# One-hot products a step ahead of the sums, and batch norm's operands loaded early, in the expert block of a four-block Flamingo kernel

## The chip, the cores and the metric

The kernel runs on one core of one Trainium2 chip. The metric is the device time of one execution in microseconds. The profiled execution, the source of all views below, is a separate run with a time of its own. The engines are called as the profile calls them: PE does matrix products, DVE and POOL elementwise work, ACT functions and copies, SP issues most of the DMAs.

## The reference, cut to what matters

The input is x of 8 sequences by 512 tokens by 256 features, with a context of the same shape. Four blocks follow each other: an mLSTM cell across to the context, a 32-head self-attention with a mixture of experts, a 16-head cross attention, and the block that the change is about, a feed-forward layer of 4096 tiny experts chosen by product keys:

```python
q = jnp.einsum('bnd,de->bne', x, w_q)
mean = jnp.mean(q, axis=(0, 1))
var = jnp.var(q, axis=(0, 1))
q = (q - mean) * jax.lax.rsqrt(var + BN_EPS) * bn_gamma + bn_beta
q = q.reshape(b, n, 2, H, KD).transpose(2, 0, 1, 3, 4)
sim = jnp.einsum('pbnhd,hkpd->pbnhk', q, keys)
sx, ix = jax.lax.top_k(sim[0], TOPK)
sy, iy = jax.lax.top_k(sim[1], TOPK)
all_scores = (sx[..., :, None] + sy[..., None, :]).reshape(b, n, H, TOPK * TOPK)
all_indices = (ix[..., :, None] * NUM_KEYS + iy[..., None, :]).reshape(b, n, H, TOPK * TOPK)
scores, pk = jax.lax.top_k(all_scores, TOPK)
indices = jnp.take_along_axis(all_indices, pk, axis=-1)
wd = down_embed[indices]
wu = up_embed[indices]
h = jnp.einsum('bnd,bnhkd->bnhk', x, wd)
h = gelu_new(h)
h = jax.nn.softmax(scores, axis=-1) * h
out = jnp.einsum('bnhk,bnhkd->bnd', h, wu)
```

H is 8, TOPK 8, NUM_KEYS 64, so a token takes 64 of 4096 experts. In front of the layer x is layer-normed, and behind it its result is scaled by the tanh of a gate and added to x. Batch norm's mean and variance run over all tokens of all sequences, so no key can be compared before the last token's features exist.

## The kernel before

Tokens come in 32 tiles of 128, and in 16 blocks of 256 (two tiles). The first 3153 us are the attention phase, blocks 1 to 3, one sequence after the other in the order 0, 4, 1, 5, 2, 6, 3, 7. There a small planner on the host interleaves lanes of work, by credits, beside the attention heads. Its last part for each sequence is `leave`: it writes x to x_d, transposes the normed features, stores them to xT_d, and adds to `gram`, the sum over tokens of feature times feature with a column of sums beside it. A lane `inner` computes, for every token of a sequence that has left and for all 4096 experts, the product of the features with `down` (`expert_products`, L123), and stores it to h_d. For the last sequence this is done in block 4. The two blocks of this last sequence are the first that block 4 works on.

Block 4 doesn't gather rows. It weighs all 4096 experts for each token, with zeros for those not chosen, and has two parts.

`fold_phase` (L1145 to L1280) makes the keys. From `gram` and w_q it takes the mean and mean square of each of the 2048 queries (y L1199, sq L1208: products of z = y times w_q with a column of ones), then a scale and shift per query (bn_sc, the power on POOL L1221), and multiplies them into the keys (ks L1226, kh L1228). pw (L1256) is w_q times these keys, copied to mk; pc (L1232) is the constant, kept in crow. From then on a similarity needs only features times mk plus crow. Between these stand the pieces of `activations`: products of the last sequence's features with four rows of down (dwl, L123 into ps_hl), and their gelu on ACT into gs. Its operands lie in up_sb, the 64 KB per partition that later hold `up`, the second table of the experts; as they are used up, `up` is loaded over them.

The step loop (L1372 on) has 128 steps (p, u): tile p, and u one of its four groups of 16 columns; eight steps make a block. The parts that a tile passes through are:

- `similar` (L1062): PE makes the similarities of a tile in two halves from features loaded from xT_d, ACT copies them to sim (L1064).
- `top` (L1075, L1076): DVE takes the eight largest of 64 for each of 16 lists, with their places. `choose` (L1082 to L1096): DVE adds the two lists, takes the eight largest of 64 again, ACT takes the exponentials. `places` (L1106 to L1142): the chosen numbers and weights, as one-hot sums on DVE, with copies on ACT (iv, kf, mlw); PE transposes them (tr), ACT copies that into ciT and cwT.
- `one_hot` (L1303 to L1309), per step: DVE writes two tables of zeros and ones (o1, o2), ACT copies the first (m1), POOL multiplies the second by the weights (m2). Each of these four has two buffers.
- `weights_of` (L1319): PE multiplies m2 by m1 into cf, the weights of all 4096 experts. `weigh` (L1328): DVE multiplies cf into gs, the activations of this block.
- `finish` (L1337): PE sums gs times up_sb over the experts, 64 rows for a block, into acc; `store` (L1352) adds x and writes out.
- `fetch` (L1360) loads a quarter of the products of the next block but one from h_d into gs, of which there are two; `apply` (L1366) takes their gelu on ACT.

Only PE's instructions are in the order of the program. DVE's, ACT's, POOL's and SP's are set by the scheduler from the order of the calls and from its own estimates. In the fold phase SP's are in program order too. In the step loop a step makes, in this order, cf of its own step, the one-hot tables of the next one, a chunk of the sums of the block before, and the weighing. Then, for a later tile, top in steps 0 and 1, choose in 2, places in 3, similar in 2 and 3, and so on for the second tile.

Of the kernel before, what the change touches and what calls it, by code (L numbers as in the profile page):

```python
# [21 lines left out]
P = 128  # L22
# [14 lines left out]
def kernel(  # L37
# [43 lines left out]
    nc.scalar.activation(tg, tg, AF.Tanh)  # L81

# [45 lines left out]

    def attention_phase(ctx: ExitStack):
# [3 lines left out]
        trp = ctx.enter_context(tc.tile_pool(name="trp", bufs=1))  # L133
        cxp = ctx.enter_context(tc.tile_pool(name="cxp", bufs=1))
        prb = ctx.enter_context(tc.tile_pool(name="prb", bufs=4))
        cel = ctx.enter_context(tc.tile_pool(name="cel", bufs=2))
        row = ctx.enter_context(tc.tile_pool(name="row", bufs=1))
        osb = ctx.enter_context(tc.tile_pool(name="osb", bufs=1))
        wmp = ctx.enter_context(tc.tile_pool(name="wmp", bufs=1))
        wsp = ctx.enter_context(tc.tile_pool(name="wsp", bufs=2))  # L140
        exp = ctx.enter_context(tc.tile_pool(name="exp", bufs=2))
# [22 lines left out]
        class Weights:  # L164


            def __init__(self, name, uses):
                self.name, self.uses, self.next = name, list(uses), None
                self.fetch()

            def fetch(self):
                self.next = None
                if self.uses:
                    w, i = self.uses.pop(0)
                    self.next = wsp.tile([P, NK, D], F32, name=self.name, tag=self.name)
                    nc.sync.dma_start(self.next, w[i].rearrange("(k p) n -> p k n", p=P))
# [7 lines left out]
        weights1 = Weights("ws1", M * [(w0, 0), (w0, 1), (w0, 2)])  # L184
        operand = [(w0, 3), (w3, 1), (w3, 0)]
        weights2 = Weights(
            "ws2", (M - 2) * (operand + [(w3, 2)]) + 2 * operand + 2 * [(w3, 2)]
# [270 lines left out]
        def cell(m):  # L458
            b = order[m]
            qn = tok.tile([P, NC, D], F32, name="qn", tag="t1")  # L460
# [64 lines left out]
            hk = tok.tile([P, NC, D], F32, name="hk", tag="t1")  # L525
# [92 lines left out]
        def queries(m):  # L618
            xn = tok.tile([P, NC, D], F32, name="xn", tag="t1")
# [39 lines left out]
        def experts(m):  # L659
# [8 lines left out]
            x2 = tok.tile([P, NC, D], F32, name="x2", tag="t2")  # L668
# [57 lines left out]
        def operands(m):  # L726
            Xb, cT = xbs[m][:, :, :D], cTs[m]
            b = order[m]
            xn = tok.tile([P, NC, D], F32, name="xn3", tag="t2")
# [43 lines left out]
        def leave(m):  # L773
# [4 lines left out]
            yield ("rest", ("H", m - 1))  # L778
            oT = exp.tile([P, NK, S], F32, name="oT3", tag="xT", bufs=1)
# [12 lines left out]
            xT4 = xTs[m] = exp.tile([P, NK, S], F32, name="xT4", tag="xT", bufs=1)  # L792
            yield from to_features(xT4, Xb)
            nc.sync.dma_start(xT_d[:, :, b * S : (b + 1) * S], xT4)
# [72 lines left out]
        def behind():  # L867
            for m in range(M):
# [3 lines left out]
                ready.add(("C", m, 0))  # L872
                for n in (m,) if m < M - 2 else (m - 1, m) if m == M - 1 else ():
                    yield ("rest", ("C", n - 1, 0))
                    yield from values1(n)
                    ready.add(("v1", n))
# [140 lines left out]
    p2 = ctx.enter_context(tc.tile_pool(name="p2", bufs=1))  # L1017
    NB = NT // 2
    up_sb = p2.tile([P, 64, D], F32, name="up_sb")
# [25 lines left out]
    tk = ctx.enter_context(tc.tile_pool(name="tk", bufs=2))  # L1045
    oh = ctx.enter_context(tc.tile_pool(name="oh", bufs=2))
    ps_t = ctx.enter_context(tc.tile_pool(name="ps_td", bufs=2, space=PSUM))

    sims, tops, chosen, cts, hots, accs = {}, {}, {}, {}, {}, {}

    def similar(p, h):

        if h == 0:
            t = tiles[p]
            xt = tk.tile([P, NK, P], F32, name="xTt")
            nc.sync.dma_start(xt, xT_d[:, :, t * P : (t + 1) * P])
            sims[p] = (xt, tk.tile([P, 16, 64], F32, name="sim"))
# [87 lines left out]
    def fold_phase(ctx: ExitStack):  # L1145

        wp = ctx.enter_context(tc.tile_pool(name="wp", bufs=2))
        st = ctx.enter_context(tc.tile_pool(name="st", bufs=1))
        ps_h = ctx.enter_context(tc.tile_pool(name="ps_hl", bufs=2, space=PSUM))
        ps_y = ctx.enter_context(tc.tile_pool(name="ps_yf", bufs=2, space=PSUM))  # L1150
        ps_s = ctx.enter_context(tc.tile_pool(name="ps_st", bufs=1, space=PSUM))

        def room(i, shape):

            axes = dict(zip("ab", shape))
            return up_sb[:, 4 * i : 4 * i + 4, :].rearrange(
                "p x y -> p (x y)"
            ).rearrange("p (a b) -> p a b", **axes)

        xl = room(15, (NK, S))  # L1160
        nc.sync.dma_start(xl, xT_d[:, :, last * S : (last + 1) * S])
        bn_sb = st.tile([P, 32], F32, name="bn_sb")
        nc.scalar.dma_start(bn_sb, bn)
        wqs = [room(n4, (NK, 512)) for n4 in range(4)]
        for n4, wq in enumerate(wqs):
            nc.scalar.dma_start(
                wq, pwq[:, 512 * n4 : 512 * (n4 + 1)].rearrange("(k p) n -> p k n", p=P)
            )
        kT = room(14, (16, 64))
        nc.scalar.dma_start(kT, keysT)  # L1170
        wTs = [room(6 + i, (4, D)) for i in range(4)]
        for i, wT in enumerate(wTs):
            nc.scalar.dma_start(wT, pwqT[:, 4 * i : 4 * i + 4, :])

        def activations(i4):

            dw = wp.tile([P, NK, 4, 64], F32, name="dwl")
            nc.sync.dma_start(dw, down[:, :, 4 * i4 : 4 * i4 + 4, :])
            for i2 in range(2):
                ps = ps_h.tile([P, 2, 2 * P], F32, name="ps_hl")  # L1180
# [265 lines left out]
```

## Time and profile before

| | us |
|---|---|
| median of 3 runs (lowest, highest) | 4202.37 (4200.03, 4207.3) |
| the profiled execution, its time | 4210.22 |
| its span | 4208.4 |
| attention phase, ends at | 3153.4 |
| fold phase, to the first one-hot product | 182.4 |
| first block, to the first store | 93.2 |
| 13 blocks, 53.4 each | 694.6 |
| last two blocks | 84.8 |

Over the span PE is busy 87%, DVE 55%, ACT 41% and POOL 14%, with a mean granted PE clock of 0.936. A time of a row in the profile is that of one instruction or group; a wait is read as "who waits, on which line, for whom". Busy shares of the whole span say little about block 4, for it is a quarter of the time and DVE is its second full engine.

### The profile page before, as it was taken

The page shows a single profiled execution, that of the slowest core. Times are in us where ns is not written, and L with a number is a line of the kernel's source. Part 1 is how long each engine was busy: PE and PEld are TensorE (multiplying, and loading weights), DVE is VectorE, ACT ScalarE, POOL GpSimd, SP SyncE. Part 2 cuts the span into 40 slices and gives each one's busy share as a digit, 9 for nine tenths or more (in the row PEclk, how much of TensorE's full clock was granted, in tenths as well). Part 3 has the DMA queues.
Part 4 walks back from the last instruction along what each step waited for, and adds up shares of the span by engine and source line. Part 5 has one row for each costly group of instructions (what it writes and reads, how often), then busy time and mean ns, then how long its engine had stood idle before and what let it go on. Part 6 is the DMA issues. An engine that isn't in the chain of part 4 may idle for free.

```text
span 4208.4 us, 75108 instructions
## 1 busy us (share of the span) xinstructions
PE 3661.8 (87%) x30633; PEld 1884.0 (45%) x30633; DVE 2332.0 (55%) x5610; ACT 1730.6 (41%) x2290; POOL 604.0 (14%) x611
## 2 busy tenths in 40 slices
PE   5588888889989989998989998788998589999998
PEld 2222343434334344434434434234445367777776
DVE  3465654455555455455545534554203488888984
ACT  2124443334544453453454443443431244554541
POOL 3210102020011012002100200100000122222221
PEclk7578999999999999999999999999998799999999
DMA  3201122123114213311421421102242422222221
GB/s 100 50 26 41 30 63 67 50 69 104 57 56 127 78 59 106 106 39 57 130 74 44 119 82 38 37 24 76 94 127 74 103 80 90 96 97 96 97 96 34
DMA packets 197477, 314.86 MB, mean 75 GB/s; under 512 B 24510, under 2 KB 149982, under 8 KB 188830
## 3 DMA queue, kind: packets, MB, share of 16 engines
q1 hardware_dynamic: 178844, 248.39, 20.0%
q0 software_dynamic: 15616, 56.63, 4.5%
q10 hardware_dynamic: 2672, 5.04, 0.4%
q8 instruction: 241, 3.95, 0.4%
q14 instruction: 104, 0.85, 0.1%
HBM read 220.93 MB, written 88.24 MB: 73 GB/s over the span
## 4 chain that ended last, share of the span: by engine, by line
PE 69%; DVE 19%; DMA 4%; issue 4%; ACT 2%; POOL 1%; SPq 0%; DVEq 0%; POOLq 0%; ACTq 0%
PE sc L333 21%; PE ps_hd L123 9%; PE acc L1337 9%; DVE nm L351 8%; PE av L394 6%; PE ps_y L710 3%; PE ps_p L282 3%; PE ps_q L293 3%; PE ps_h L693 3%; PE csc L567 2%; PE cav L552 2%; PE ps_sim L1062 1%; DVE gs L1328 1%; PE cf L1319 1%; PE ps_hl L123 1%
## 5 line engine op out<-in xcount | busy, mean ns | idle before, releaser
L351 DVE TENSOR_REDUCE nm<-sc 128x2 f32<-128x1024 f32 x768 | 939.7, 1225 | 1020.6 <-PE sc L333 1016.9
L379 ACT ACTIVATE pr<-sc 128x1024 f32<-128x1024 f32 x768 | 785.1, 1023 | 1043.5 <-PE sc L333 1041.8
L333 PE MATMUL sc<-ka,qa 32*128 32x512 f32 x3072 | 938.7, 673 | 216.4 <-DVE nm L351 201.8
L333 PE MATMUL sc<-qa,ka 32*128 32x512 f32 x3072 | 897.4, 657 | 22.7 <-ACT pr L379 11.4
L333 PEld LDWEIGHTS sc<-ka,qa 32*128 32x128 f32 x3072 | 256.4, 191 | 626.4 <-DVE nm L351 431.2
L1337 PE MATMUL acc<-up_sb,gs 64*128 64x256 f32 x4096 | 493.0, 396 | 39.3 <-DVE gs L1328 39.3
L1337 PEld LDWEIGHTS acc<-up_sb,gs 64*128 64x128 f32 x4096 | 407.3, 196 | 95.7 <-DVE gs L1328 41.4
L123 PE MATMUL ps_hd<-xT,dw 128*64 128x256 f32 x3584 | 432.2, 385 | 4.8 <-DVE pd L572 2.1
L394 PE MATMUL av<-pr,v 128*32 128x512 f32 x3072 | 427.2, 629 | 4.7 <-ACT pr L379 4.7
L123 PEld LDWEIGHTS ps_hd<-xT,dw 128*64 128x64 f32 x3584 | 244.9, 137 | 231.6 <-issue 105.8
L1309 POOL TENSOR_TENSOR m<-o,cwT 128x1024 f32<-128x1024 bf16 x128 | 244.3, 1909 | 693.5 <-PE cf L1319 444.9
L333 PEld LDWEIGHTS sc<-qa,ka 32*128 32x128 f32 x3072 | 242.3, 187 | 68.9 <-issue 33.6
L826 ACT COPY hb<-ps_hd 128x512 f32<-128x512 f32 x224 | 130.7, 585 | 293.3 <-PE ps_hd L123 279.3
L545 ACT ACTIVATE pd<-mb,aT 128x512 f32<-128x512 f32 (+3 forms) x256 | 129.7, 553 | 206.3 <-PE cav L552 94.8
L394 PEld LDWEIGHTS av<-pr,v 128*32 128x32 f32 x3072 | 61.5, 109 | 310.4 <-issue 292.0
L537 POOL TENSOR_SCALAR_AFFINE_SELECT mb<-mb 128x256 f32<-128x256 f32 x128 | 52.2, 408 | 864.5 <-DMA mb<-nM_d 439.8
L1319 PE MATMUL cf<-m,m 64*64 64x64 f32 x8192 | 152.6, 222 | 23.6 <-DVE gs L1328 23.5
L572 DVE SCALAR_TENSOR_TENSOR pd<-csc,pd 128x512 f32<-128x512 f32 (+3 forms) x256 | 115.6, 484 | 95.8 <-PE csc L567 72.0
L1328 DVE TENSOR_TENSOR gs<-cf,gs 128x1024 f32<-128x1024 f32 x128 | 154.7, 1209 | 15.4 <-PE cf L1319 15.4
L1319 PEld LDWEIGHTS cf<-m,m 64*64 64x64 f32 x8192 | 135.8, 135 | 58.8 <-issue 54.6
L567 PE MATMUL csc<-qT,cT 32*128 32x256 f32 (+3 forms) x512 | 148.8, 561 | 12.5 <-DVE pd L572 9.0
L1075 DVE MAX8 s<-sim 128x8 f32<-128x64 f32 x512 | 91.1, 210 | 117.0 <-ACT sim L1064 117.0
(225 smaller groups left out, 4212.5 us busy)
## 6 DMA issues: line engine op xcount, KB each, us to landing
h_d<-hb SPq DMA_DIRECT2D x224, 256.0 KB
gs<-h_d SPq DMA_DIRECT2D x56, 1024.0 KB
dw<-in_down SPq DMA_DIRECT2D x112, 256.0 KB
w1e<-in_w POOLq DMA_DIRECT2D x16, 1024.0 KB, 5.5
w2e<-in_w POOLq DMA_DIRECT2D x16, 1024.0 KB, 6.0
mb<-nM_d SPq DMA_DIRECT2D x32, 512.0 KB
qk_d<-pk SPq DMA_DIRECT2D x64, 256.0 KB
ws<-in_w SPq DMA_DIRECT2D x56, 256.0 KB
```

Source lines behind the costliest of these rows:

```text
L123: nc.tensor.matmul(ps[64 * q : 64 * q + 64, :], dw[:, k, :], runs[:, :, q, :], start=(k == 0), stop=(k == NK - 1),)
L333: nc.tensor.matmul(sc[:, i, :], lhs[r : r + 32, g, c * P : (c + 1) * P], rhs[r : r + 32, g, :], start=True, stop=True,)
L351: newest = nc.vector.tensor_reduce(self.nm[:, c, 2 * half : 2 * half + 2, g], sc, AX.X, ALU.max, negate=True)
L379: nc.scalar.activation(self.pr[jj], sc, AF.Exp)
L394: nc.tensor.matmul(self.av[32 * j : 32 * j + 32, :], self.va[:, c, h * (self.hd + 1) : h * (self.hd + 1) + 32], pr[j // 2][:, j % 2, :], s ...
L545: nc.scalar.activation(pds[c][:, i, s0:], mb[:, i, s0:], AF.Exp, bias=aT[:, c, h : h + 1])
L567: nc.tensor.matmul(sc[i][:, s0:], cT[r : r + 32, g, s0 : s0 + P], qT[r : r + 32, g, s0:], start=True, stop=True,)
L826: nc.scalar.copy(hb.rearrange("p n i t -> p i n t"), ps.rearrange("p i (n t) -> p i n t", n=2),)
L1309: nc.gpsimd.tensor_tensor(m2, o2, tokens(cw), ALU.mult)
L1319: nc.tensor.matmul(cf[64 * q : 64 * q + 64, h, s, :], m2[rows, 4 * q + s // 2, :, s % 2], m1[rows, 4 * q + s // 2, :, s % 2], start=True, ...
L1328: nc.vector.tensor_tensor(gv, cf.rearrange("p h s i -> p i h s"), gv, ALU.mult)
L1337: nc.tensor.matmul(accs[n][q], gs[n % 2][rows, i, :], up_sb[rows, i, :], start=(i == 0), stop=(i == 63),)
```

## The change

Of the attention phase: the pools that are used only early move to the other end of SBUF, and are closed when the last sequence's operands are made. The room is given at once to up_sb, and SP loads into it w_q in both layouts (pwq, pwqT), the keys and four pieces of down. The last sequence's transposed features are written straight to their place in up_sb, rather than to xT_d and back, and its last part no longer waits for the expert products of the sequence before it. `bn` is loaded at the start.

Of the fold phase: y is made with the queries in rows (32 products of 128x257, w_q stationary, gram moving). DVE multiplies by the other layout and reduces, so that the 64 products sq with a column of ones are gone; ACT copies the mean column. The expert products come in 32 pieces that are put between the other steps as fill, with down loaded four pieces ahead, into rows 48 to 55 of up_sb. ps_hl and y have three PSUM buffers instead of two. Two more tiles' worth of similarities are made here (tiles 2 and 3). Pools in block 4 wait for a buffer tile by tile.

Of the step loop: the one-hot tables are made two steps ahead, and cf one step ahead of the step that weighs it. PE then has cf of the next step, then a chunk of sums. Top, choose and places of a block's two tiles come in the block before, and their similarities at steps 6 and 7 of the block before that, with the features loaded at steps 3 and 4. Fetches are at steps 1, 2, 4 and 5, gelus at 3, 4, 6 and 7, the store at step 6, and the sums are cut differently.

```diff
+    class Fold:
+        def load(self):
+            pool = ctx.enter_context(tc.tile_pool(name="ups", bufs=1, side="right"))
+            self.up = pool.tile([P, 64, D], F32, name="up_sb")
+            self.xl = self.room(15, (NK, S))
+            self.wqs = [self.room(n4, (NK, 512)) for n4 in range(4)]
+            for n4, wq in enumerate(self.wqs):
+                nc.sync.dma_start(
+                    wq, pwq[:, 512 * n4 : 512 * (n4 + 1)].rearrange("(k p) n -> p k n", p=P)
+                )
+            self.wTs = [self.room(6 + i, (4, D)) for i in range(4)]
+            for i, wT in enumerate(self.wTs):
+                nc.sync.dma_start(wT, pwqT[:, 4 * i : 4 * i + 4, :])
+            self.kT = self.room(14, (16, 64))
+            nc.sync.dma_start(self.kT, keysT)
+            self.dws = {}
+            for i4 in range(4):
+                self.fetch(i4)
...
@@ leave @@
-            yield ("rest", ("H", m - 1))
+            if m < M - 1:
+                yield ("rest", ("H", m - 1))
+                oT = exp.tile([P, NK, S], F32, name="oT3", tag="xT", bufs=1)
+            else:
+                oT = fold.room(10, (NK, S))
...
+            else:
+                yield from to_features(fold.xl, Xb)
@@ behind @@
+                if m == M - 1:
+                    early.close()
+                    fold.load()
@@ fold_phase @@
+        mv = st.tile([P, 16, 2], F32, name="mv")
+        for n4 in range(4):
+            z = room(4 + n4 % 2, (4, D))
+            for i in range(4):
+                n = 4 * n4 + i
+                y = ps_y.tile([P, 512], F32, name="y", tag="y")[:, : D + 1]
+                for k in range(NK):
+                    nc.tensor.matmul(
+                        y, fold.wqs[n4][:, k, i * P : (i + 1) * P], gram[:, k, :],
+                        start=(k == 0), stop=(k == NK - 1),
+                    )
+                nc.vector.tensor_tensor(z[:, i, :], y[:, :D], wTs[n4][:, i, :], ALU.mult)
+                nc.scalar.copy(mv[:, n, 1:2], y[:, D : D + 1])
+            nc.vector.tensor_reduce(mv[:, 4 * n4 : 4 * n4 + 4, 0], z, AX.X, ALU.add)
+        fill(4)
...
         for h in range(2):
+            pw = [ps_y.tile([P, 8, 64], F32, name="pw", tag="y") for _ in range(NK)]
...
+            fill(2)
+            similar(0, h)
+            top(0, 8 * h)
+        values(2, 0, 1, 3, 4)
+        for h in range(2):
+            similar(1, h)
+        choose(0)
+        fill(6)
+        places(0)
+        values(5)
+        for h in range(2):
+            top(1, 8 * h)
+        choose(1)
         for h in range(2):
             similar(2, h)
+        fill(8)
+        for h in range(2):
+            similar(3, h)
+        places(1)
+        fill(32)
+        values(6, 7)
@@ the step loop, all of it @@
-    one_hot(0, 0)
-    cuts = (0, 11, 22, 33, 44, 54, 64)
-    for p in range(NP):
-        n = p // 2
-        for u in range(4):
-            step = 4 * (p % 2) + u
-            cf = weights_of(p, u)
-            if p + u // 3 < NP:
-                one_hot(p + u // 3, (u + 1) % 4)
-            if n > 0 and step < 6:
-                finish(n - 1, cuts[step], cuts[step + 1])
-            weigh(p, u, cf)
-            if p + 2 < NP:
-                if u < 2:
-                    top(p + 2, 8 * u)
-                elif u == 2:
-                    choose(p + 2)
-                else:
-                    places(p + 2)
-            if p + 3 < NP and u >= 2:
-                similar(p + 3, u - 2)
-            if n > 0 and step == 5:
-                store(n - 1)
-            if n > 0 and n + 1 < NB and step in (2, 3, 4, 5):
-                fetch(n + 1, step - 2)
-            if n > 0 and n + 1 < NB and step >= 4:
-                apply(n + 1, step - 4)
+    cuts = (0, 11, 22, 33, 44, 55, 64, 64, 64)
+    steps = [(p, u) for p in range(len(tiles)) for u in range(4)]
+    for step in steps[:2]:
+        one_hot(*step)
+    ahead = weights_of(*steps[0])
+    for g, (p, u) in enumerate(steps):
+        n, step = g // 8, g % 8
+        cf, ahead = ahead, weights_of(*steps[g + 1]) if g + 1 < len(steps) else None
+        weigh(p, u, cf)
+        if n > 0:
+            finish(n - 1, cuts[step], cuts[step + 1])
+        if g + 2 < len(steps):
+            one_hot(*steps[g + 2])
+        if n > 0 and step == 6:
+            store(n - 1)
+        if n + 1 < NB:
+            q = 2 * n + 2 + step // 4
+            if u < 2:
+                top(q, 8 * u)
+            elif u == 2:
+                choose(q)
+            else:
+                places(q)
+        if n + 2 < NB:
+            if step in (3, 4):
+                features(2 * n + 1 + step)
+            if step >= 6:
+                for h in range(2):
+                    similar(2 * n - 2 + step, h)
+        if n > 0 and n + 1 < NB:
+            if step in (1, 2, 4, 5):
+                fetch(n + 1, (1, 2, 4, 5).index(step))
+            if step in (3, 4, 6, 7):
+                apply(n + 1, (3, 4, 6, 7).index(step))
```

## The prediction

> **What bounds the kernel now.** I read busy time by windows first. The page's slices end in a stretch where DVE goes to 8 and 9 tenths; I cut it where block 4 begins (first product of dwl, 3153.4), at the first one-hot product (3335.8), at the first store's sum (3429.0) and before the last two blocks (4123.6).
>
> ```profile
> core 0: us, PE busy (x) PEld busy (x) DVE busy (x) ACT busy (x) POOL busy (x), PEclk, DMA share, GB/s
> 3153.40:3335.80 182.40, 126.50 (x776) 78.91 (x776) 56.33 (x237) 35.41 (x92) 8.32 (x5) 0.80 0.40 102
> 3429.00:4123.60 694.60, 640.58 (x10306) 490.39 (x10302) 613.93 (x2549) 346.98 (x519) 197.95 (x104) 0.96 0.29 95
> ```
>
> The fold phase is a third idle on PE, with its clock at 0.80. The steady loop is 13 blocks of 53.4 us, PE 92% and DVE 88% busy: both are nearly full. Next the waits, first of the fold phase:
>
> ```profile
> POOL bn_sc L1221 <- DVE bn_sc L1220: 65.7, 1, 65.7
> PE ps_hl L123 <- DMA dwl<-in_down: 25.1, 2, 15.9
> PE ps_sim L1062 <- DMA xTt<-xT_d: 15.5, 1, 15.5
> ```
>
> PE stands for transfers: of dwl 25.1 us, of the features xTt 15.5 us. Then the waits of the loop (3480 to 4120, 12 blocks):
>
> ```profile
> ACT gs L1366 <- DMA gs<-h_d: 41.8, 17, 4.6
> PE acc L1337 <- DVE gs L1328: 33.4, 12, 2.8
> PE cf L1319 <- DVE gs L1328: 14.4, 12, 1.2
> ```
>
> Per block PE waits 2.8 us once for the last weighing, and 1.2 once. The timeline of PE shows the place and what follows:
>
> ```profile
> 3641.49 1.19 PE L1319 MATMUL cf<-m,m 64*64 64x64 f32 x64 [1.20 <-DVE gs L1328]
> ...
> 3649.11 8.07 PE L1337 MATMUL acc<-up_sb,gs 64*128 64x256 f32 x44 [2.79 <-DVE gs L1328]
> ```
>
> 44 sums take 8.07 us after that wait, 4.95 at full clock (the same 44 elsewhere in that timeline): the window 3648.5 to 3655.3 has clock 0.50. So a block is 256 sums 28.8 + 8 cf x 1.12 = 9.0 + four similarity products 8.8 + two tr 0.8 = 47.4, waits 4.0, lost clock 2: 53.4.
>
> Last, DVE and POOL together:
>
> ```profile
> 3585.13 1.90 POOL L1309 TENSOR_TENSOR m<-o,cwT 128x1024 f32<-128x1024 bf16 x1 [3.79 <-ACT gs L1366]
> 3585.64 1.47 DVE L1129 TENSOR_TENSOR mlw<-w,sm 128x64 f32<-128x64 f32 x1
> ```
>
> The 128x64 product takes 1.47 us here and 0.23 alone: it ends when POOL's product does.
>
> **What the Trainium skill says.** "SBUF — State Buffer", section "Who interferes with whom": a DVE instruction with two SBUF inputs and a GpSimd instruction that reads SBUF block each other for a whole instruction. The pair above agrees. "TensorE: Matmul & The Clock Gate", Part 1: an idle window of 3.4 us halves the clock. Here waits of 2.8 us already brought 0.50, for 6.8 us and in another block for 3.4 us. Same page, "Engine queue depths": ACT and DVE are strictly first in, first out; the order below rests on it. "Trainium Kernel Development and Optimization", "Key Constraints": queues of different engines share the 16 DMA engines, so a transfer isn't faster for coming from another queue. Agrees: dwl is waited for while the ups move at 221 to 233 GB/s.
>
> **The change part by part.** *Loads in the attention phase.* Now 5.6 MB are issued on SP at about 2876; at 190 to 237 GB/s (the trace's heavy stretches) 24 to 30 us, ahead of the last ws, xT_d and h_d on SP. Those come due over 25 us later; their order on all engines is the same up to the last leave. I take 0, bounds 0 and +5 (beyond that, the fourth rival). The last element's transposed features stay on chip, which removes its store and reload, hence the 15.5, and its transposes stand before 72 expert products: block 4 begins 1.2 us sooner.
>
> *Fold phase, PE at full clock.* y: 64 rows x 0.26 (ps_g, same form) 16.7. Thirty-two pieces of expert products (8 of L123) at 1.88: 60.2. pw 7.4, pc twice 0.9, eight similarity products at 2.2 = 17.6, two tr 0.8. Sum 104.5 (before 126.5 busy at a mean clock of 0.80, with six similarity products). The 64 small sums of squares are gone; the 4 reductions and 16 column copies on DVE and ACT are under y. The chain bn_sc to ks (POOL's pow 2.9, ks 1.1, five small ones) is about 5.5, covered by four pieces (7.5). Down pieces are fetched four deep; the ninth and tenth of 256 KB queue behind 5.2 MB of ups (22 to 25 us), of which the eight pieces and two products in front hide all but 6.6. Other stalls (ACT's copies, choose and places ahead of tr) 4. Half clock after them 3. Sum 118: first cf at 3152.2 + 118.5 = 3270.7, so 65 earlier than 3335.8. Bounds 105 (no stalls) and 140 (ups at 150 GB/s).
>
> *First block.* Its sums end after one block of steps with DVE in front (50, below) and the first steps of the next (34): 84 after the first cf, before 93.2. So 74 us are gained by 3354.6, 3429.0 before. Range 52 to 88.
>
> *Loop, PE.* The same 47.4 per block; cf a step ahead takes away the 1.2 and 2.8 and their half clock, if the weights are there.
>
> *Loop, DVE and ACT.* Only PE is in program order; DVE's and ACT's order in the built program decides. Before, top, choose and places (two tiles: 10.6 + 6.7 + 7.3 = 24.6) were spread over all eight steps. After, DVE has all 24.6 between the weighing of step 7 and the weighing of step 3, and only one-hots and weighings in steps 4 to 7. ACT has mlw's copy of the second tile and the first two gelus ahead of the m1 copy for step 5, and the m1 copy for step 0 of the next block behind the gelus of the third fetch. So each block holds a ring, in which no step can begin before the one ahead of it:
> (1) DVE, from o1 of step 2 (made two steps ahead, behind the weighing of step 6 of the block before) to the end of step 3's weighing: five one-hot pairs 6.0, fin 0.9, five weighings at 1.13 = 5.6, and the 24.6: 37.1. The POOL products of these five pairs hold DVE's two-input operations, 1.25 each as for L1129 (1.47 - 0.23): 6.2; ACT's replies 0.5. Together 43.8.
> (2) ACT: mlw's copy 0.35, a table load 1.28, two gelus 1.94 and m1 of step 5 1.04, less the weighing of 1.13 that runs beside it: 3.5.
> (3) PE: cf of step 5 1.1 and the 44 rows of step 4's sums 5.0: 6.1. These read the rows that the third fetch fills.
> (4) The third fetch from h_d 5.5 (3616.5 to 3621.5 before, 5.0, and its wait), its two gelus 1.94, and m1 of step 0 1.04: 8.5. Only now is the buffer free in which o1 of step 2 is made: back at (1).
> Sum 61.9. Behind each cf on PE stand that step's sums and all later ones. PE stands some 8 us for the weighing of step 2 (at cf of step 4) and 3 to 4 for m1 (at cf of step 5); the half clock after it that falls into (3) adds 0 to 1.5. I take 62.4 against 53.4: 9.0 x 13 blocks = +117. The last two blocks have no fetch, and one has no top: -1. The store a step later, the features' loads (256 tokens' 256 KB at steps 3 and 4, used at 6 and 7, some 12 us later against 5 for a fetch) and bn's 16 KB at the start cost nothing under this; the last ups are due only with the first sums, a block after they are issued. PSUM buffers that wait tile by tile move no work; were the features late, PE would wait at L1062, 5 us at most. POOL's holds are bounded by 0 (ring 56) and 1.9 each (ring 65); queues that overlap better than written, as ACT's replies in (2), may save 2.
>
> Sum against the profiled execution (4210.2, span 4208.4, 1.8 around it): 4210.2 - 74 + 117 - 1 = 4252. The median of the runs shown is 7.8 lower: 4244. The break-even is a ring of 53.4 + 75/13 = 59.2.
>
> **Rivals.** *Faster, the ring is not closed:* DVE keeps ahead in its light half, since the gelu copies and fetches come before their turn in the ring; the loop goes at PE's pace, 47.4 to 49. For: DVE's own work is 44.1 a block, below PE's 47.4. Against: that 24.6 stands in one half, and that the holds are measured. Time 4202 - 74 - 13 x 5 = 4063. Its place is (1), where DVE would have to be a step ahead when top begins; it decides the sign once the ring falls below 59.2, 3.2 us less than my sum. Chance 0.11.
> *Faster, by the fold alone:* the ring is 54.5 to 58.5, as most of the holds fall on operations with one input (MAX8) and vanish. 4202 - 75 + 13 x 3.1 = 4167. For: L1303's mean of 0.75 in the loop is only 0.07 above its median. Chance 0.11.
> *No difference that can be measured:* ring within 0.6 of 59.2, 4202, chance 0.05.
> *Slower than forecast:* the stalls of 8 and 4 bring half clock for 6.8 us each time, or the loads hold SP and the last attention waits 15 to 25: 4244 + 40 = 4284. For: the 6.8 measured. Chance 0.10.
> The forecast itself: 0.63, with its own range 4218 to 4268.
>
> **How the numbers follow.** About 0.2% (8 us) is what a measurement of this kernel can tell from no change. Slower takes the forecast and the last rival, 0.73; the same 0.05; faster 0.22. The range leaves out the first rival and part of the last: from 4150, which takes in most of the second, to 4285.
>
> **What would show it.** Right: first cf near 3271; block stores 61 to 63.5 apart; in the waits PE cf <- DVE gs of about 8 and PE cf <- ACT m of 3 to 4 us per block, at steps 4 and 5, where L1337's waits were; DVE without idle from weighing 7 to weighing 3; ACT's gelus waiting for h_d just before m1. Wrong: stores under 59 apart, or a first cf after 3290, or attention's end moved by more than 5.

## The result, and the profile after

The changed kernel takes 4180.12 us (4171.26 to 4183.94, 5 runs) against 4200.03 (4190.99 to 4207.3, 5 runs beside it): ratio 0.9951, 95% interval 0.9932 to 0.9971. It is faster by half a per cent, where 4244 and slower were forecast. The profiled execution took 4180.12 (span 4178.2), 30 below that of before.

The profile after in windows: attention phase to the first y, fold phase to the first cf, first block to its store, 13 blocks, the rest. The columns are those of the windows before.

```profile
core 0: us, PE busy (x) PEld busy (x) DVE busy (x) ACT busy (x) POOL busy (x), PEclk, DMA share, GB/s
0.00:3139.57 3139.57, 2745.30 (x17189) 1204.48 (x17190) 1550.31 (x2437) 1300.41 (x1605) 356.60 (x482) 0.95 0.25 73
3139.57:3256.50 116.93, 100.79 (x691) 62.62 (x689) 84.49 (x397) 45.81 (x121) 7.41 (x3) 0.96 0.36 83
3256.50:3340.30 83.80, 66.60 (x1299) 52.00 (x1301) 73.25 (x216) 30.65 (x49) 30.22 (x15) 0.84 0.23 68
3340.30:4095.50 755.20, 656.81 (x10337) 500.81 (x10329) 630.25 (x2550) 311.55 (x494) 204.18 (x104) 0.93 0.26 88
```

The fold phase takes 116.9 where it took 182.4: 65.5 won. The first block takes 83.8 where it took 93.2: 9.4 won. Thirteen blocks take 755.2, 58.1 each, where they took 694.6: 60.6 lost. The rest takes 82.7 against 84.8: 2.1 won. That leaves 16.4 won in block 4. The attention phase ended 13.8 sooner in this execution (3153.4 to 3139.6). Of that 1.2 was expected of the change, and the rest can't be told from the spread of this phase: in the profiles of eleven kernels here that all have this attention phase, the first y comes anywhere from 3129.5 to 3162.8. So the fold and the loop are compared below, and not the two spans; and 16.4 + 1.2 = 17.6 agrees with the 20 between the medians.

The waits of the steady loop after (3340 to 4080), who waits for whom, us in total, times, longest:

```profile
ACT gs L1421 <- DMA gs<-h_d: 81.0, 25, 5.8
DVE o L1358 <- ACT m L1360: 63.6, 24, 2.9
PE cf L1374 <- ACT m L1360: 54.9, 12, 5.3
PE cf L1374 <- DVE gs L1383: 31.9, 13, 2.5
```

PE's waits for the last weighing in front of the sums, 33.4 before, are gone. In their place PE waits once a block 4.6 for m1 and once 2.5 for a weighing, both at cf, as the forecast had it in kind. The sizes differ: it had 3 to 4 and 8.

One turn of the ring, in the timeline after (start, us, engine, line, and in brackets the idle time before it and what ended it), from o1 of step 2 to the next o1 of step 2:

```profile
3629.82 0.69 DVE L1358 TENSOR_TENSOR o<-ciT,iota 128x1024 bf16<-128x1024 bf16 x1 [2.43 <-ACT m L1360]
...
3643.21 1.90 POOL L1364 TENSOR_TENSOR m<-o,cwT 128x1024 f32<-128x1024 bf16 x1 [4.32 <-DVE s L1139]
3643.77 0.34 DVE L1156 MAX8 psc<-al 128x8 f32<-128x64 f32 x2
...
3644.42 0.33 DVE L1156 MAX8 psc<-al 128x8 f32<-128x64 f32 x2
...
3649.30 3.00 DVE L1180 TENSOR_TENSOR hot<-kf,iota 128x512 bf16<-128x512 bf16 x2
...
3665.19 2.60 DVE L1180 TENSOR_TENSOR hot<-kf,iota 128x512 bf16<-128x512 bf16 x2
...
3669.71 1.21 DVE L1383 TENSOR_TENSOR gs<-cf,gs 128x1024 f32<-128x1024 f32 x1
...
3673.39 1.98 ACT L1360 CAST m<-o 128x1024 f32<-128x1024 bf16 x2
3674.52 1.98 PE L1374 MATMUL cf<-m,m 64*64 64x64 f32 x64 [3.94 <-ACT m L1360]
3676.43 6.41 PE L1392 MATMUL acc<-up_sb,gs 64*128 64x256 f32 x44
3679.90 8.57 SPq L1415 DMA_DIRECT2D gs<-h_d  x2
3684.57 2.00 ACT L1421 ACTIVATE gs<-gs 128x1024 f32<-128x1024 f32 x2 [5.59 <-DMA gs<-h_d]
3686.48 1.03 ACT L1360 CAST m<-o 128x1024 f32<-128x1024 bf16 x1
3687.54 0.69 DVE L1358 TENSOR_TENSOR o<-ciT,iota 128x1024 bf16<-128x1024 bf16 x1 [2.29 <-ACT m L1360]
```

The turn is 57.7, the four legs of the forecast's ring in its order, and two of them are shorter than it had them. Leg (1), 3629.82 to 3670.84, where DVE goes on from the weighing to its next instruction, is 41.0 and not 43.8: POOL's product in the line at 3643.21 lies over MAX8 and FIND_INDEX8, which go on at their usual pace (0.65 for two lists, under the product and without it); only where it meets `hot` does DVE wait (3.00 and 2.60 for two products that take 1.29 alone). This agrees with the Trainium skill ("SBUF — State Buffer", "Who interferes with whom"): a DVE instruction with at most one SBUF input, outside DVE's two-port modes, does not contend with GpSimd. Leg (2), to the end of m1, is 3.6 (forecast 3.5). Legs (3) and (4) up to the gelus are 10.1 and not 6.1 + 5.5 and half a clock: SP issues the fetch at 3679.90, while the sums of that chunk go on to 3682.77. It overwrites rows 32 to 47, and the chunk of step 4 sums 44 to 54, so only four of its eleven rows are in the way. The seven others are 2.9 us that the fetch does not wait for, and from its issue to its gelus it takes 4.7 and not 5.5; against this, half clock stretches cf and the whole chunk from 6.1 to 8.4. The gelus and m1 are 2.97 (forecast 3.0).

### The profile page after: what moved, and what is told of

It reads as the page before. It is cut to its first block, busy times and chain, and to the rows that moved or that the text cites. A ratio compares the mean times of both kernels' runs of the same rounds, so it can differ in the third digit from the quotient of the medians.

```text
span 4178.2 us, 74949 instructions
## 1 busy us (share of the span) xinstructions
PE 3636.0 (87%) x30537; PEld 1877.8 (45%) x30537; DVE 2363.8 (57%) x5622; ACT 1698.3 (41%) x2282; POOL 612.5 (15%) x611
## 4 chain that ended last, share of the span: by engine, by line
PE 62%; DVE 24%; ACT 4%; DMA 4%; issue 4%; POOL 1%; SPq 0%; DVEq 0%; POOLq 0%; ACTq 0%
PE sc L378 21%; PE ps_hd L125 9%; DVE nm L396 9%; PE av L439 6%; PE acc L1392 4%; PE ps_y L755 3%; PE ps_q L338 3%; PE ps_p L327 3%; PE ps_h L738 3%; PE csc L612 2%; PE cav L597 2%; DVE i L1140 2%; DMA gs<-h_d 2%; DVE hot L1180 2%; DVE gs L1383 1%
## 5 line engine op out<-in xcount | busy, mean ns | idle before, releaser
L1364 POOL TENSOR_TENSOR m<-o,cwT 128x1024 f32<-128x1024 bf16 x128 | 253.0, 1978 | 713.6 <-PE cf L1374 472.8
L1374 PE MATMUL cf<-m,m 64*64 64x64 f32 x8192 | 171.1, 237 | 110.8 <-ACT m L1360 65.3
L1374 PEld LDWEIGHTS cf<-m,m 64*64 64x64 f32 x8192 | 153.4, 150 | 147.7 <-issue 145.6
L1358 DVE TENSOR_TENSOR o<-ciT,iota 128x1024 bf16<-128x1024 bf16 x128 | 105.6, 825 | 95.8 <-ACT m L1360 74.1
```

What stands on the lines that cost most here:

```text
L1364: nc.gpsimd.tensor_tensor(m2, o2, tokens(cw), ALU.mult)
L1374: nc.tensor.matmul(cf[64 * q : 64 * q + 64, h, s, :], m2[rows, 4 * q + s // 2, :, s % 2], m1[rows, 4 * q + s // 2, :, s % 2], start=True, ...
```

## The experiments

All ran beside the kernel before. The theory is the forecast's ring with the two corrected legs. Times are medians; "blocks" is the distance of stores, the mean of 13.

| run | us | ratio to before (95%) | blocks |
|---|---|---|---|
| changed kernel | 4180.1 | 0.9951 (0.9932 to 0.9971) | 58.1 |
| fold_only | 4119.5 | 0.9788 (0.9759 to 0.9817) | 53.6 |
| loop_only | 4266.5 | 1.0127 (1.0100 to 1.0153) | 58.1 |
| cuts12 | 4167.0 | 0.9898 (0.9876 to 0.9920) | 56.4 |
| pool_eighth | 4126.5 | 0.9830 (0.9797 to 0.9863) | 54.8 |
| rows_late | 4183.2 | 0.9958 (0.9941 to 0.9974) | 58.0 |
| rows_late2 | 4254.6 | 1.0119 (1.0098 to 1.0140) | 62.3 |
| late_load | 4180.8 | 0.9944 (0.9927 to 0.9960) | 58.0 |
| late_load2 | 4195.5 | 0.9994 (0.9983 to 1.0005) | 58.0 |
| ahead_only | 4131.1 | 0.9836 (0.9803 to 0.9869) | 54.5 |
| hand | 4336.6 | 1.0307 (1.0285 to 1.0330) | 68.3 |
| hand2 | 4174.6 | 0.9932 (0.9908 to 0.9955) | 56.6 |
| hand3 | 4089.6 | 0.9722 (0.9691 to 0.9753) | 50.6 |

### The two parts apart

fold_only puts the step loop of before (the block marked - in the diff above) into the changed kernel, with one edit:

```diff
-            if p + 3 < NP and u >= 2:
+            if p > 0 and p + 3 < NP and u >= 2:
+                if u == 2:
+                    features(p + 3)
                 similar(p + 3, u - 2)
...
```

> The attention and fold parts of the change with the step loop of before (features of tile 3 come from the fold phase, as there). If the two parts are independent: first cf at 3256 to 3270 as in the changed kernel, blocks 53.4 apart as before, the whole some 67 us below before (65.5 in the fold phase, 1.4 in the tail of the attention phase): about 4133. Rival, that the fold's gain needs the new loop (ups or similarities late for the old one): less than 40 us gained.

loop_only puts the new step loop behind the old fold phase, which makes the similarities of tiles 2 and 3 as well; its pools wait tile by tile as in the changed kernel.

> The fold phase of before, with two more similarities at its end, and the new step loop. If the loss is the loop's own: blocks 58 apart, 13 x 4.65 = 60 us lost, 9 gained in the first block, 4 lost by the similarities: about 4200 + 55 = 4255. Rival, that the new loop is slow only behind the new fold phase: blocks at 53 to 54, within 15 us of before.

The windows of fold_only: fold phase, first block, 13 blocks.

```profile
3145.30:3262.90 117.60, 101.42 (x691) 62.85 (x689) 84.53 (x397) 45.82 (x121) 7.42 (x3) 0.94 0.36 82
3262.90:3336.70 73.80, 65.16 (x1316) 49.80 (x1314) 71.40 (x213) 34.22 (x53) 28.95 (x15) 0.88 0.32 91
3336.70:4033.10 696.40, 634.82 (x10304) 486.61 (x10297) 618.00 (x2549) 345.10 (x519) 204.50 (x104) 0.96 0.29 95
```

The blocks are those of before. The fold phase gains 64.8, and the first block 19.4 more: 90 in all between the medians, where I had written 67 (of the 89 between the two profiles, 8 lie in the end of the attention phase, and blocks and end take 3 back). The 19.4 are as long as a wait of the kernel before that comes twice in its first block and has no counterpart in fold_only:

```profile
PE tr L1136 <- ACT mlw L1133: 19.4, 2, 11.2
```

There the similarities of tile 2 ended the fold phase and those of tile 3 came in the loop, so that DVE chose for them while PE stood. In the new fold phase both stand ahead of the last expert products. In the changed kernel the new loop takes 10 of the 19.4 back.

loop_only has blocks of 58.1 and loses 57: the loop is slow by itself, whatever is in front of it. So the change is a gain of some 85 (64.8, 19.4 and the 1.2) and a loss of some 68 (60.6 in 13 blocks, 10 in the first block, 2 less at the end), and each comes without the other. By the medians the two runs add up to 33 less where the changed kernel has 20 less; the spread of the attention phase is of that size, and the 13 were not followed further.

### What is in the ring: the third fetch

cuts12 lets the third fetch go a step earlier:

```diff
-    cuts = (0, 11, 22, 33, 44, 55, 64, 64, 64)
+    cuts = (0, 12, 24, 36, 48, 56, 64, 64, 64)
...
-            if step in (1, 2, 4, 5):
-                fetch(n + 1, (1, 2, 4, 5).index(step))
+            if step in (1, 2, 3, 5):
+                fetch(n + 1, (1, 2, 3, 5).index(step))
```

> The changed kernel with sums cut at 12, 24, 36, 48, 56, 64 instead of 11, 22, 33, 44, 55, 64 and the third fetch issued at step 3: row 48, the last that the third fetch overwrites, is then summed in front of cf of step 5 and not behind it. Ring theory: the leg from m1 of step 5 through cf and four rows of sums to the fetch and its gelus (10.1 us) leaves the ring, and the next chain (cf, two chunks of 8 rows, weighing of step 6) is some 3 to 4 us shorter: blocks at 54 to 55.5 apart, about 4137. Rival, that DVE's 24.6 us in one half bound the loop and the fetch only happens to end there: blocks within 1 us of 58.1, 4170 to 4185.

Blocks are 56.4 apart, between the two expectations: 1.7 comes free, half of what I had written. In its trace the third gelus wait for nothing, and m1 of step 0 waits for cf of step 6 instead, which frees its buffer; the scheduler had also given DVE and ACT another order, so that this run alone does not show that the fetch was in the ring.

rows_late does the opposite and sums seven rows ahead of the four that the fetch waits for:

```diff
-        for i in range(i0, i1):
+        for i in (*range(48, 55), *range(44, 48)) if i0 == 44 else range(i0, i1):
```

> The changed kernel with one chunk of sums in another order: in step 4 rows 48 to 54 and then 44 to 47, where it was 44 to 54. The third fetch overwrites rows 32 to 47, so it now waits for the whole chunk, as the forecast had it for the changed kernel. If the ring is what the forecast says, and its leg (3) was only too long by the seven rows that the fetch does not wait for: their time at half clock (6.4 of 11 rows, so some 3 us) comes back in every block: blocks 61 apart, 13 x 3 = 40 more, about 4220. Rival, that the third fetch is off the path: blocks 58.1, 4180.

Nothing changed, and read alone this would say that the fetch is off the path. It does not: the scheduler had answered with another order on ACT. In the timeline of rows_late, m1 of step 0 (3640.14) stands ahead of the third gelus:

```profile
3640.14 1.05 ACT L1360 CAST m<-o 128x1024 f32<-128x1024 bf16 x1 [4.80 <-PE cf L1374]
3643.68 2.01 ACT L1421 ACTIVATE gs<-gs 128x1024 f32<-128x1024 f32 x2 [2.50 <-DMA gs<-h_d]
```

rows_late2 has the same sums, with the third gelus called ahead of that copy and the copy held behind them, so that ACT, DVE and POOL have the changed kernel's order, instruction for instruction:

```diff
-        nc.scalar.copy(m1, o1)
+        with tc.issue_after(gelus.pop().ins) if gelus else nullcontext():
+            nc.scalar.copy(m1, o1)
...
```

> The changed kernel with rows 48 to 54 summed ahead of 44 to 47 in step 4, as in the run before with these rows, where the scheduler had answered by moving the m1 copy of step 0 in front of the third fetch's gelus on ACT; here that copy is held behind those gelus, so that the orders of ACT, DVE and POOL are the changed kernel's. The run with the other order had the gelus 2.8 us later and blocks still 58.0 apart. If the ring is the forecast's, with m1 of step 0 behind the third fetch: blocks 58.1 + 2.8 to 3.1 = 61 apart, 13 x 3 = 39 above 4180, about 4219. Rival, that the fetch has slack in either order: 58.1, 4180.

The same place in its timeline:

```profile
3658.99 5.57 PE L1393 MATMUL acc<-up_sb,gs 64*128 64x256 f32 x44
3664.64 5.55 SPq L1416 DMA_DIRECT2D gs<-h_d  x2
3669.55 2.00 ACT L1422 ACTIVATE gs<-gs 128x1024 f32<-128x1024 f32 x2 [8.01 <-DMA gs<-h_d]
3671.46 1.97 ACT L1361 CAST m<-o 128x1024 f32<-128x1024 bf16 x2
```

The fetch now comes after the whole chunk, and blocks are 62.3 apart, 4.2 more (3 expected): the ring goes through the third fetch, and a transfer late by seven rows of sums is paid in every block. This is the forecast's ring with its own leg (3): it had 62.4 a block and 4244, and this kernel has 62.3 and 4254.6. (Of its 74 over the changed kernel the blocks and the first block make 58; in the profile the rest lies ahead of the first y, 3156.7 for 3139.6.) So that leg is a step that failed: with the fetch behind the whole chunk the forecast's sign would have come out. That its size does too is partly luck, for the holds here are still the smaller ones. The two runs also bear out the fixed order on ACT that the forecast rests on: m1 of step 0 came late only where it stood behind the gelus.

### What is in the ring: POOL's holds

pool_eighth has POOL multiply an eighth of each table, into two fixed buffers, and leaves out the other seven eighths of the weights:

```diff
...
-        m2 = oh.tile([P, 8, 64, 2], F32, name="m2")
-        nc.gpsimd.tensor_tensor(m2, o2, tokens(cw), ALU.mult)
+        m2 = m2s[(4 * p + u) % 2]
+        nc.gpsimd.tensor_tensor(m2[:, 0:1], o2[:, 0:1], tokens(cw)[:, 0:1], ALU.mult)
```

> The changed kernel with POOL's product m2 of an eighth of its size into two fixed buffers set to zero before the loop; seven eighths of the experts' weights are left out. What POOL holds of DVE goes (3.6 us of the stretch from o1 of step 2 to the weighing of step 3, by the trace of the changed kernel: two first products of hot at 3.0 and 2.6 for 1.3 each, one o1). Ring theory: blocks 58.1 - 3.6 = 54.5 apart, 13 x 3.6 = 47 less, about 4133. The forecast's own figure for the holds was 6.2: then 51.9, 4100. Rival, that ACT and the fetch bound the ring without DVE: 58, 4180.

Blocks are 54.8 apart, 3.3 less, and the median 54 less: 43 in 13 blocks, and 12 in the first block (71.6 for 83.8). The products of hot, in the groups of pool_eighth by line (count, busy, mean ns of one):

```profile
L1180 DVE TENSOR_TENSOR hot<-kf,iota 128x512 bf16<-128x512 bf16 x52 | 32.8, 670 | 0.0
```

and of the changed kernel:

```profile
L1180 DVE TENSOR_TENSOR hot<-kf,iota 128x512 bf16<-128x512 bf16 x52 | 61.9, 1230 | 0.0
L1159 DVE TENSOR_TENSOR w<-psc 128x64 f32<-128x64 f32 x26 | 16.8, 647 | 0.0
```

29.1 us in 13 blocks, 2.2 each, went from this row alone, and w went from 647 ns to 204, another 0.44 per tile, two tiles a block. The holds are on the ring, about one for one: 3.3 a block came free where the trace of the changed kernel had 3.6 of them, and the forecast 6.2. In the kernel before hot takes 0.69 and is not held; there POOL met other instructions.

### Where the fold phase's gain comes from

late_load issues the 5.6 MB for block 4 at its start in the program, not in the attention phase.

> The changed kernel with the loads of w_q, its other layout, the keys and the first four pieces of down (5.6 MB) issued by SP when block 4 begins, not in the attention phase. If PE's waits for transfers are what the fold phase lost before: y waits for the first w_q and DVE for the layouts, 5.6 MB at about 220 GB/s are 25 us, of which the 14.4 us of y and what can follow hide some: first cf 15 to 25 later, about 4195 to 4205. Rival, that the gain is in the new order of the pieces and fewer products alone: within 5 us of 4180.

The scheduler moved these loads back, 2867.5 to 2879.7 in the trace (2862.3 to 2874 in the changed kernel). So the run tests nothing; it is the changed kernel once more, and shows how well it repeats: 4180.8 and 4180.1. late_load2 ties each load to gram:

```diff
+                nc.vector.tensor_copy(wq[:, 0, 0:1], gram[:, 0, 0:1])
                 nc.sync.dma_start(
...
```

> As the run with late loads, in which the scheduler had moved the loads back to where they were (2867 to 2879), so that it was the changed kernel once more; now each load first has one column of its place written by DVE from gram, so that none can begin before gram is complete. 5.6 MB at 220 GB/s are 25 us: y waits 4 for the first w_q, DVE for the layouts until 14, the first piece of down comes at 24 to 26 where it was wanted at 14.4. If only that counts: first cf some 10 later than the 117 us after y that it takes in the changed kernel, 4190. If the waits for transfers of before (25.1 and 15.5) were taken away by the early loads: 30 to 40 later, 4215. If the loads collide with nothing: 4180.

The timeline of PE in late_load2, where y begins:

```profile
3142.06 4.53 PE L1269 MATMUL y<-gram,up_sb 128*128 128x257 f32 x12 [3.19 <-DMA up_sb<-in_pwq]
3148.56 13.24 PE L1269 MATMUL y<-gram,up_sb 128*128 128x257 f32 x52 [1.97 <-ACT mv L1274]
```

From the end of gram's products (3138.9) to the first cf (3265.2) it is 126.4, where the changed kernel has 116.9: early loads are worth 9.5 of the 65.5 in this trace (15 between the medians, with the spread of the attention phase in it). That is the first case of the expectation, but not by its working: the loads moved at 381 GB/s (3142 to 3155) and not 220, so that PE waited 3.2 and 2.0 at y, as shown, with half clock between, and for down only 1.9 (1.8 in the changed kernel). The rest is the order and the work of the fold phase. PE's groups of that phase before, with what they waited for:

```profile
L123 PE MATMUL ps_hl<-up_sb,dwl 128*64 128x256 f32 x512 | 68.2, 431 | 30.9 <-DMA dwl<-in_down 25.1 <-ACT gs L1185 5.8
L1208 PE MATMUL sq<-ones,up_sb 128*128 128x1 f32 x64 | 10.5, 259 | 2.7 <-DVE up_sb L1203 2.7
L1208 PE MATMUL sq<-gram,up_sb 128*128 128x1 f32 x64 | 10.4, 266 | 0.0
```

and after:

```profile
L125 PE MATMUL ps_hl<-up_sb 128*64 128x256 f32 x512 | 58.9, 388 | 14.2 <-ACT gs L1230 12.4 <-DMA up_sb<-in_down 1.8
L1262 PE MATMUL y<-gram,up_sb 128*128 128x257 f32 x64 | 14.3, 382 | 0.1
```

20.9 us of products with one column are gone (y itself was 14.8). The expert products take 9.3 less, at a better clock (388 ns each for 431). PE's idle time falls from 55.9 to 16.1, by 23.3 in waits for down, 15.5 for the features and 6.9 for kh in front of pc, less 6.6 more for gelus on ACT. How much of these 23.3 is due to loads four deep, and how much to the ups behind them, was not tried apart.

### What is good in the loop, and what isn't

ahead_only has the new fold, the loop of before, and only the products ahead:

```diff
-            cf = weights_of(p, u)
-            if p + u // 3 < NP:
-                one_hot(p + u // 3, (u + 1) % 4)
+            cf, ahead = ahead, None
+            if 4 * p + u + 1 < 4 * NP:
+                ahead = weights_of(p + u // 3, (u + 1) % 4)
+            if p + u // 2 < NP:
+                one_hot(p + u // 2, (u + 2) % 4)
...
```

> The new fold phase with the step loop of before, and of the loop's change only this: the one-hot tables are made two steps ahead and cf one step ahead of the weighing; top, choose, places, similarities, fetches, gelus and the store stay at the steps of before. If the loss is the place of top, choose and places in one half and not the products ahead: PE's waits for the weighing (1.2 and 2.8 a block) and the half clock after them go, DVE's 44.1 with some 4 of POOL's holds sets the pace, blocks at 49.5 to 52 apart, 13 x 2.5 = 32 below the fold alone, 4075 to 4095. Rival, that cf a step ahead closes the ring by itself (m1 behind gelus behind fetches): blocks at 56 or more, 4155 or more.

Neither came: blocks of 54.5, 0.9 above fold_only. The waits for the last weighing in front of the sums are gone, but DVE is now 94% busy, and cf waits 5.4 once a block for a weighing (70.3 us in 13 waits). POOL's product now meets other instructions of DVE: o1 takes 1051 ns on average where it takes 775 in fold_only, o2 854 for 682, w 1405 for 348, which is 4.5 us a block with the 1.2 that mlw's product gains taken off. So of the new loop's 4.6 a block about 1 belongs to the products ahead, and 3.6 to the rest of the loop's change, as far as two runs can be subtracted. That this is the place of top, choose and places is argued and not shown: similarities, fetches, gelus, the store and the shares of the sums moved too, and were not taken apart.

hand gives DVE and ACT of the loop the order of the program, which spreads top, choose and places over eight steps:

```diff
+    ctx.enter_context(
+        tc.manual_schedule(engines={mybir.EngineType.PE, mybir.EngineType.DVE, mybir.EngineType.Activation})
+    )
```

> The changed kernel, with DVE's and ACT's instructions in the step loop in program order as PE's are: top, choose and places of a block's two tiles are then spread over all eight steps. If it is their place in one half that makes the ring: PE sets the pace, blocks at 50 to 52 apart, 4180 - 13 x 7 = about 4090. Rival, that DVE and ACT in strict program order wait for each other's replies (exp, kf, mlw, gelus waiting for fetches) more than they win: blocks at 56 or more, 4155 or more.

Blocks of 68.3: the rival's case. The timeline shows two queues, on PE and on DVE:

```profile
3768.09 0.90 PE L1200 MATMUL tr<-ident,mlw 128*128 128x128 f32 x3 [10.63 <-ACT mlw L1197]
3777.39 1.22 DVE L1386 TENSOR_TENSOR gs<-cf,gs 128x1024 f32<-128x1024 f32 x1 [9.75 <-ACT gs L1424]
```

PE, in program order too, stands for a tr that DVE has only just been asked for, and the gelus stand behind places' copies on ACT. hand2 takes tr and its copies out of places into a function of their own, called a step later, and has similarities and gelus ahead of top, choose and places in each step:

```diff
+    def turn(p):
+        mlw = mlws.pop(p)
         tr = ps_t.tile([P, 4, P], F32, name="tr", tag="s")
...
+        if g >= 4 and u == 0 and g // 4 + 1 < len(tiles):
+            turn(g // 4 + 1)
```

> The changed kernel with DVE and ACT of the step loop in program order as in the run before with that order, but tr and its copies a step after places, gelus and similarities in front of top, choose and places, and the copies of the chosen numbers made with choose. There the blocks were 68.3 apart, with PE 10.6 for tr behind places and DVE 9.8 for the last gelus, which stood behind places' copies on ACT. If those two queues were the loss and the spread itself is good: 68.3 - 10.6 - 5.0 (tr's second wait) = 52.7 or less, blocks at 49 to 53, 4178 - 13 x 7 = 4065 to 4115. Rival, that strict program order costs elsewhere as much as it saves: blocks at 56 or more, 4150 or more.

Blocks of 56.6 and not 49 to 53: the two waits are gone, and among the waits of the loop DVE has none left. Its timeline shows why it needs so long; each MAX8 here is followed by the FIND_INDEX8 that needs it:

```profile
3757.77 0.21 DVE L1139 MAX8 s<-sim 128x8 f32<-128x64 f32 x1
3758.23 0.21 DVE L1139 MAX8 s<-sim 128x8 f32<-128x64 f32 x1
3758.68 0.21 DVE L1139 MAX8 s<-sim 128x8 f32<-128x64 f32 x1
```

0.457 a list. In the changed kernel the scheduler had put two MAX8 in front of their two FIND_INDEX8, 0.65 for two lists. hand3 writes it so:

```diff
-        for n in range(n0, n0 + 8):
-            sim = sims[p][1][:, n, :]
-            nc.vector.max(out=s8[:, n, :], in_=sim)
-            nc.vector.max_index(out=i8[:, n, :], in_max=s8[:, n, :], in_values=sim)
+        for n2 in range(n0, n0 + 8, 2):
+            for n in (n2, n2 + 1):
+                nc.vector.max(out=s8[:, n, :], in_=sims[p][1][:, n, :])
+            for n in (n2, n2 + 1):
+                nc.vector.max_index(
+                    out=i8[:, n, :], in_max=s8[:, n, :], in_values=sims[p][1][:, n, :]
+                )
...
```

> The second kernel with DVE and ACT in program order, with each list of DVE's top and choose taken in pairs: two MAX8, then their two FIND_INDEX8, and the same for the one-hot sums of places. In that kernel DVE is never idle: 56.6 a block, with 0.457 us for a list where MAX8 and FIND_INDEX8 alternate against 0.327 in the changed kernel where they come in pairs; 48 lists a block are 6.2 us. If DVE's own time bounds it: 56.6 - 6.2 = 50.4 apart, 13 x 6.2 = 81 below, about 4094. Rival, that another wait takes its place (m2, tr, the fetch): 54 or more, 4140 or more.

The window of its 13 blocks:

```profile
3350.60:4008.10 657.50, 630.63 (x10326) 480.32 (x10330) 632.18 (x2548) 346.23 (x521) 213.93 (x105) 0.98 0.30 101
```

50.6 a block, PE and DVE both 96% busy, PE's clock 0.98. At 4089.6 it is faster than both kernels, 2.8% below before (0.9722, 0.9691 to 0.9753). So the idea of the new loop is sound once DVE's work is spread over the block: DVE has 2548 instructions in 13 blocks of either kernel, in another order, and the blocks are 50.6 for 58.1 apart. Whether the loop of before would gain as much from a written order was not tried.

## Why the prediction was wrong

*The attention phase*: not contradicted, and not shown. A cost of the loads, and the 1.2 gained, are both hidden by a spread of 33 in the end of that phase; the end moved by 13.8, which the forecast had named as a sign of being wrong, but with this spread it tells nothing. The loads' own time was put too long: they moved at 370 GB/s (2866 to 2882), some 16 us, and not at 190 to 237. That the profiled execution of before was taken as it stands made no error, since all sums were differences within block 4.

*The fold phase*: right in the sum, in part by luck. First cf 118.5 after y forecast, 116.9 measured. In its terms: expert products 60.2 forecast and 58.9 measured, y 16.7 and 14.3, all of PE's work 104.5 and 100.8, stalls with half clock 13.6, and 16.1 of idle time measured. The wait put down to down's ninth piece behind the ups was 1.8 and not 6.6; instead PE stood 12.4 for gelus on ACT, so that two errors of opposite sign nearly cancel. The forecast also took dwl's wait as agreeing with queues that share the DMA engines; dwl and the ups are both issued by SP, so no trace here tests that.

*The first block*: right, 84 and 83.8.

*The loop*: this is where the forecast failed. The mechanism was right, the ring with its four legs and the third fetch, and PE's stalls at cf of steps 4 and 5. Two terms of its sum were too large. In leg (1) POOL's five holds at 1.25 each, 6.2, taken from a two-input product; the stretch has 3.9 over DVE's own 37.1, holds and replies together, since most of POOL's product lies over MAX8 and FIND_INDEX8. In leg (3) all eleven rows of step 4's sums stood ahead of the third fetch; four do. Leg (3) up to the gelus of (4) is 2.0 shorter: 2.9 for the rows and 0.8 in the fetch, less 1.8 for half clock beyond the 0.5 that the forecast had. Together that is 2.8 + 2.0, 57.7 for 62.4. With 58.1 a block the loop costs 60.6, not 117, and the break-even of 59.2, which was right, lies between the two rings. A ring 4.3 us too long on 62.4 turned the sign, because it recurs 13 times against a gain that comes once.

The rival "faster, by the fold alone" is what happened: its range of 54.5 to 58.5 holds the 58.1, and its reason, that POOL's holds fall on operations with one input, is the first of the two terms. It had 4167. I had the evidence for it in the same text (o1's mean only 0.07 above its median) and gave it 0.11.

## What to carry to other kernels

Work out a ring leg by leg, and ask at every leg what the next instruction really reads or overwrites: a transfer waits for the last row that it overwrites, not for the group of instructions that this row stands in (here 3679.90 and not 3682.77). Where a gain comes once and a loss recurs, compare the error of the recurring term, times its count, with the margin before giving a sign. If only one engine is in written order, look at what the scheduler did to the others before judging a change of order, in the experiments too: it undid one of these runs and masked another.

## What was not expected of the hardware

MAX8 and FIND_INDEX8 on DVE cost 0.457 us a list when each FIND_INDEX8 follows the MAX8 that it needs, and 0.33 when two and two are grouped. With 48 lists a block this is 6.3 us, and blocks went from 56.6 to 50.6, with no instruction added or taken away (the same edit also pairs the one-hot sums of places). The Trainium skill ("VectorE: DVE Perf Modes", "The DRAIN you can't avoid") reports eight copies in which a semaphore after each costs nothing extra. These lists are another case: the time is lost where a short instruction stands right behind the one whose result it needs. Whether the semaphore or the emptying of the engine makes up the 0.13 was not tried.

Half clock came after short waits of PE. In the changed kernel the second wait of a block, 3.6 to 5.3 us, brought it in all 13 blocks (in the turn above cf took 1.98 instead of 1.19, and 44 products 6.41 instead of 5.02). The first wait, 2.5 us, brought it in 6 of 13. In hand3 it came after six waits of 2.1 us, for 3.4 us each time, and did not come after three others of 2.1 or 2.2.
